# A windowed linear-attention layer: reciprocal denominators spread by transfers through memory and multiplied in by GpSimd, in place of matrix products and VectorE

## The chip, the core and the metric

The kernel runs on one core of one Trainium2 chip. The metric is the device time of one execution in microseconds (us); lower is better. Each line number is that of the kernel before, unless it is said to be of the changed kernel.

## The reference, cut to what matters

The network has two layers on an image of 256 channels and 64 x 64 pixels. Only layer 0 is touched. It is a linear attention with eight heads of 32 channels, over boxes of three sizes around each pixel:

```python
q = sigmoid(Wq x); k = sigmoid(Wk x); v = (Wv x) / |Wv x|        # x group-normed
for w in (1, 2, 4):                                              # box side 64, 32, 16
    wk, wkv = box(integral(k)), box(integral(k * v))             # sums over the box
    attn = einsum('bdhw,bdfhw->bfhw', q, wkv)                    # 32 channels of a head
    norm = einsum('bdhw,bdhw->bhw', q, wk)                       # one number a head and pixel
    outs.append(attn / (norm[:, None] + 1e-06))                  # <- the division
x = x + Wout @ concat(outs) + bout
```

Layer 1 (attention over all pixels, then a mixture of experts) follows and is the same in both kernels.

## The kernel before

The 4096 pixels are kept as 8 vertical strips (`NCH`) of 512 pixels (`CH`). The heads are done in two groups of four (`KC` = 2, loop at L744), since four heads fill 128 partitions. For each group `prepare` (L304) makes q, k, v, the box sums of k and, from them, all denominators of the group: the tile `den`, 128 x 512, whose row 32·(i mod 4) + 4·(2w + i div 4) + h holds the denominators of window w, strip i and head h. L526 adds 1e-6 and L527 takes all reciprocals at once, into the tile `rec`.

`attend` (L581) then works the three windows in the order w = 2, 1, 0, with reaches r = 1, 2, 4 (box half-sides in cells of 8 pixels). A window with r > 1 begins with a **band part** (L593 to L657: four bands b, products of 64 rows), and each window has a **strip part** (L660 to L708: eight strips ix). Both go in steps. One step makes for each of four heads a 128 x 512 (or narrower) product of k and q in a PSUM bank `sc` (L609, L678; six banks, four to a step). `masked` (L545) multiplies it by a mask into the tile `sm` (twelve buffers, so three steps): VectorE does so straight from PSUM for heads 0 and 2, and for head 3 in every second step; head 1, and head 3 in the other steps, are copied to `sm` by ScalarE (L554) and multiplied there by GpSimd (L558). Two steps later TensorE multiplies v by the four `sm` (L640, L694). A strip's sum goes to the tile `raw` (L704, VectorE, or L706, ScalarE, for r = 1). There is one buffer of `raw`.

When a window is done its divisions and projections are put into the list `chores` (L737 to L741), and each step of the next window pops one (`step_done`, L538); before the next window writes `raw` again, and at the end of the group, `finish` does what is left. A **division** (L714) treats two strips: for each, TensorE multiplies a 0/1 matrix of the constants (`spread`) by 32 rows of `rec`, which puts each head's reciprocal on that head's 32 rows in a PSUM bank (L718), and VectorE multiplies `raw` by the bank (L725). A **projection** (L727) treats one strip: four products of `raw` with the output weights `woT` (L731), added to the residual `t` by VectorE (L735).

Each engine runs its instructions in an order fixed when the kernel is built, and waits in that order. The builder may place an instruction earlier on its engine than the program writes it, where its inputs are expected to be ready. SyncE's queue (SP) issues the DMAs concerned here: the weights (L203, L205), the constants (L126) and the image rows (L285).

Of the kernel before, what the change touches and what calls it, by code (L numbers as in the profile page):

```python
# [22 lines left out]
F32 = mybir.dt.float32  # L23
# [7 lines left out]
P = 128  # L31
C = 256
KC = C // P
N = 4096
NT = N // P
CH = 512
NCH = N // CH
IMG = 64
SW = 8
BH = 16  # L40
NB = IMG // BH
CELL = SW * SW
D = 32
GRP = 8
REACH = (4, 2, 1)
NW = len(REACH)
# [14 lines left out]
    "k": {"sums": NCH // 4 * NW * D, "spread": NCH // 4 * NW * P, "before8": CH, "sides": NB * (SW + IMG + 1)},  # L61
# [9 lines left out]
def constants():  # L71
# [15 lines left out]

# [3 lines left out]
    col = np.arange(P)[None, :]  # L91
    out[:, _AT["spread"]] = np.concatenate([p[:, None] % D == 4 * n + col // D for n in ns], 1)
# [19 lines left out]
def tile_conv_attn_hybrid(ctx: ExitStack, tc: tile.TileContext, a: dict, out: bass.AP):  # L112
# [27 lines left out]
    def tok(i):  # L140
        return slice(P * i, P * (i + 1))
# [44 lines left out]
    with ExitStack() as phase:  # L186
# [9 lines left out]
        big = phase.enter_context(tc.tile_pool(name="c_big", bufs=1))  # L196

        def weights(g):

            gs = slice(P * g, P * (g + 1))  # L200
            w3 = big.tile([P, KC, 3, P], F32, tag="w3", name="w3")
            for n, name in enumerate(("wqT", "wkT", "wvT")):
                nc.sync.dma_start(w3[:, :, n, :], a[name][:, gs].rearrange("(k p) o -> p k o", p=P))  # L203
            woT = big.tile([P, NW, C], F32, tag="woT", name="woT")
            nc.sync.dma_start(  # L205
                woT, a["woutT"].rearrange("(w g p) o -> p w g o", g=KC, p=P)[:, :, g, :]
            )
            return w3, woT

        with (  # L210
# [27 lines left out]
            first = weights(0)  # L238
# [65 lines left out]
        def prepare(g, prep, ps):  # L304
# [4 lines left out]
            w3, woT = weights(g) if g else first  # L309
# [217 lines left out]
            nc.vector.reciprocal(rec, rec)  # L527
# [15 lines left out]
        turns = [0]  # L543

        def masked(work, scs, used, pieces):  # L545


            turns[0] += 1
            sms = []
            for h, sc in enumerate(scs):  # L550
                sm = work.tile([P, CH], F32, tag="sm", name="sm", bufs=12)
                src, engine = sc, nc.vector
                if h == 1 or h == 3 and turns[0] % 2:
                    nc.scalar.copy(sm[:, :used], sc[:, :used])  # L554
                    src, engine = sm, nc.gpsimd
                for at, n, mk in pieces:
                    to, of = (z[:, at : at + n].rearrange("p (m n) -> p m n", n=mk.shape[-1]) for z in (sm, src))
                    engine.tensor_mul(to, of, mk.unsqueeze(1).to_broadcast(list(to.shape)))  # L558
                sms.append(sm)
            return sms  # L560
# [20 lines left out]
        def attend(g, work, ps, qk, v, ssum, rec, woT):  # L581
# [6 lines left out]
            for w in (2, 1, 0):  # L588
# [125 lines left out]
                def division(ix, raw=raw, w=w):  # L714

                    for i, by in ((ix, score()), (ix + 1, score())):
                        at, n = slice(D * (i % 4), D * (i % 4 + 1)), NCH // 4 * w + i // 4
                        nc.tensor.matmul(  # L718
                            by,
                            ck["spread"][at, P * n : P * (n + 1)],  # L720
                            rec[at, :],
                            start=True,
                            stop=True,
                        )
                        nc.vector.tensor_mul(raw[:, i, :], raw[:, i, :], by)  # L725
# [18 lines left out]
        for g in range(KC):  # L744
            with tc.tile_pool(name="c_prep", bufs=1) as prep, psum("c_ps1", 2) as ps:
                of = prepare(g, prep, ps)
            with tc.tile_pool(name="c_work", bufs=1) as work, psum("c_ps2", 1) as ps:
                attend(g, work, ps, *of)
# [753 lines left out]
```

## Time and profile before

| | |
|---|---|
| median of three runs | 2935.82 us (2933.38 to 2937.23) |
| the profiled execution's own time | 2937.02 us |
| its span | 2935.2 us, so 1.82 us lie around it |
| layer 0, group 0: `attend`, first product to last | 142.6 to 527.3 us of the span |
| layer 0, group 1: the same parts | 643 to 1029 us |
| reach 1, strip part (group 0) | 144.2 to 232.3 us |
| reach 2, band part; strip part | 232.3 to 301.6; 301.6 to 370.5 us |
| reach 4, band part; strip part | 370.5 to 447.0; 447.0 to 508.1 us |
| last divisions and projections of the group | 508.1 to 527.4 us |
| mean granted TensorE clock | 0.974 of full speed |

In the lines of the profile, L718 is line 718 of the kernel; an entry such as `ps_sc<-rec,cstk` names the tile written and those read; PE is TensorE (PEld its weight loads), DVE VectorE, ACT ScalarE, POOL GpSimd. A float32 product appears as two matmul records. "Idle before" is the time for which the engine had nothing to run just before, and the name behind the arrow is what it waited for. The matmul ends are modelled, so that a TensorE that shows as busy throughout may still hide short waits.

### The profile page before, as it was taken

To read this page: it belongs to the slowest core of one execution; us is meant where nothing else is said; L and a number is where in the kernel's file an instruction comes from. 1 tells how busy PE (TensorE), PEld (TensorE's weight loads), DVE (VectorE), ACT (ScalarE), POOL (GpSimd) and SP (SyncE) were. 2 spreads that over 40 slices of the span, in tenths; PEclk is the share of its full clock that TensorE was granted. 3 is DMA by queue.
4 is the path that set the end of the run, shared out by engine and by line. 5 is a ranking of instruction groups with operands and counts; after the bars stand their busy time and mean duration, and the time that the engine had idled before them with its cause. 6 is when DMAs were issued, how large, how long until landed. Compare 5 with 4: busy or idle time off the path is not lost. (4 is left out here: it accounts for less than half of the span.)

```text
span 2935.2 us, 63107 instructions
## 1 busy us (share of the span) xinstructions
PE 2794.7 (95%) x26358; PEld 1352.3 (46%) x26358; DVE 2083.2 (71%) x3005; ACT 1533.0 (52%) x2134; POOL 720.3 (25%) x816
## 2 busy tenths in 40 slices
PE   6899999989999989999999999999999699999996
PEld 5466442735644354222222222222222268888884
DVE  5776768577677877999999999999999821111113
ACT  3242323124233213888888888888888622222222
POOL 1085858119485621000000000000000022222220
PEclk9999999999999999999999999999999879999997
DMA  5000000000000000000000000000000155555555
GB/s 142 6 3 3 2 3 2 7 1 3 4 2 3 1 19 1 5 5 5 5 5 5 5 5 5 5 5 5 5 5 5 53 182 200 191 189 195 192 196 198
DMA packets 97930, 137.35 MB, mean 47 GB/s; under 512 B 18242, under 2 KB 79272, under 8 KB 97636
## 3 DMA queue, kind: packets, MB, share of 16 engines
q1 hardware_dynamic: 82360, 105.31, 10.9%
q0 software_dynamic: 6912, 18.88, 2.2%
q10 hardware_dynamic: 8364, 9.02, 0.9%
q8 instruction: 210, 3.44, 0.5%
q14 instruction: 84, 0.69, 0.1%
HBM read 115.07 MB, written 18.12 MB: 45 GB/s over the span
## 5 line engine op out<-in xcount | busy, mean ns | idle before, releaser
L1001 ACT ACTIVATE pe<-ps_two 128x1024 f32<-128x1024 f32 x1024 | 993.1, 1022 | 150.0 <-PE ps_two L991 145.4
L1008 DVE TENSOR_TENSOR total<-total,pe 128x1024 f32<-128x1024 f32 x928 | 1058.2, 1217 | 0.0
L991 PE MATMUL ps_two<-qk 32*128 32x512 f32 x4096 | 629.1, 639 | 3.6 <-POOLq L946 1.9
L959 PE MATMUL ps_acc<-pe,v 128*32 128x512 f32 x4096 | 546.4, 605 | 0.1
L554 ACT COPY sm<-ps_sc 128x384 f32<-128x384 f32 (+4 forms) x486 | 232.4, 512 | 459.5 <-PE ps_sc L678 276.4
L558 POOL TENSOR_TENSOR sm<-sm,mask 128x192 f32<-128x192 f32 (+3 forms) x460 | 380.2, 861 | 231.6 <-ACT sm L554 231.0
L991 PEld LDWEIGHTS ps_two<-qk 32*128 32x128 f32 x4096 | 204.8, 183 | 418.7 <-PE ps_two L991 222.2
L558 DVE TENSOR_TENSOR sm<-ps_sc,mask 128x384 f32<-128x384 f32 (+3 forms) x708 | 324.2, 518 | 91.7 <-PE ps_sc L678 90.2
L1417 ACT ACTIVATE hid<-ps_hp,cols 128x256 f32<-128x256 f32 x288 | 136.4, 473 | 382.8 <-PE ps_hp L1416 382.0
L1266 POOL MEMSET on<- 128x256 f32 x1 | 0.3, 311 | 1175.1 <-PE ps_den L959 1175.1
L959 PEld LDWEIGHTS ps_acc<-pe,v 128*32 128x32 f32 x4096 | 80.7, 108 | 389.4 <-issue 376.2
L1416 PE MATMUL ps_hp<-xe,w 128*128 128x256 f32 x1152 | 257.0, 381 | 0.0
L1423 PE MATMUL ps_yp<-w,hid 128*128 128x256 f32 x1152 | 254.6, 379 | 0.0
L678 PE MATMUL ps_sc<-qk 32*128 32x192 f32 (+3 forms) x2688 | 245.3, 446 | 5.2 <-DVE sm L558 2.9
L1423 PEld LDWEIGHTS ps_yp<-w,hid 128*128 128x128 f32 x1152 | 216.4, 190 | 28.1
L1416 PEld LDWEIGHTS ps_hp<-xe,w 128*128 128x128 f32 x1152 | 208.5, 190 | 42.1 <-ACT hid L1417 5.0
L694 PE MATMUL ps_acc<-sm,v 128*32 128x192 f32 (+3 forms) x2688 | 216.6, 423 | 0.8 <-POOL sm L558 0.8
L1395 DVE TENSOR_SCALAR xe<-ps_tp,cols 128x256 f32<-128x256 f32 x72 | 35.9, 540 | 248.8 <-PE ps_tp L1391 228.7
L558 POOL TENSOR_TENSOR sm<-sm,ycut 128x384 f32<-128x384 f32 (+4 forms) x150 | 150.7, 1025 | 140.4 <-ACT sm L554 140.2
L678 PEld LDWEIGHTS ps_sc<-qk 32*128 32x128 f32 x2688 | 126.4, 186 | 124.0 <-DVE sm L558 70.4
L1425 DVE TENSOR_TENSOR y<-ps_yp,b 128x256 f32<-128x256 f32 x72 | 30.6, 425 | 208.1 <-PE ps_yp L1423 208.1
L558 DVE TENSOR_TENSOR sm<-ps_sc,ycut 128x512 f32<-128x512 f32 (+4 forms) x250 | 127.7, 562 | 64.8 <-PE ps_sc L609 62.7
(231 smaller groups left out, 2252.5 us busy)
## 6 DMA issues: line engine op xcount, KB each, us to landing
w<-in_L_ffn_W SPq DMA_DIRECT2D x72, 1024.0 KB
b<-in_L_ffn_b SPq DMA_DIRECT2D x36, 128.0 KB
rows<-in_x SPq DMA_DIRECT2D x16, 256.0 KB
zrows<-z SPq DMA_DIRECT2D x4, 1024.0 KB
y<-yrows SPq DMA_DIRECT2D x8, 512.0 KB
y<-yrows ACTq DMA_DIRECT2D x8, 512.0 KB
rec<-recs SPq DMA_DIRECT2D x60, 64.0 KB
x<-in_x ACTq DMA_DIRECT2D x4, 512.0 KB
```

The source lines that it names most:

```text
L554: nc.scalar.copy(sm[:, :used], sc[:, :used])
L558: engine.tensor_mul(to, of, mk.unsqueeze(1).to_broadcast(list(to.shape)))
L678: nc.tensor.matmul(scs[h][:, at : at + n], kT[hs[h], tok(i)], qT[hs[h], CH * ix + CELL * c0 : CH * ix + CELL * c1], start=True, stop=True, ...
L694: nc.tensor.matmul(acc[hs[h], CELL * c0 : CELL * c1], v[:, i, hs[h]], sms[h][:, at : at + n], start=not begun[0], stop=last and at == plac ...
L959: nc.tensor.matmul(to[D * hd : D * (hd + 1), :], lhsT(hd), rhs[:, hd, :], start=start, stop=stop, skip_group_check=True,)
L991: nc.tensor.matmul(sc[hd // 2][:, hd % 2, :], qk[hs, 1, g, tok(i)], qk[hs, 0, g, chunk(qc)], start=True, stop=True,)
L1001: nc.scalar.activation(pe[:, pair, :], s, AF.Exp, scale=C**-0.5)
L1008: add = nc.vector.tensor_add(to, first[:, pair, :] if i == 1 else to, pe[:, pair, :])
L1395: nc.vector.tensor_scalar(xe[:, k, :], tp[:, k, :], cols[:, gain], cols[:, shift], op0=ALU.mult, op1=ALU.add,)
L1416: nc.tensor.matmul(hp, w1[:, k, tok(n)], x_now[:, k, :], start=k == 0, stop=k == KC - 1)
L1417: nc.scalar.activation(hid[:, n, :], hp, AF.Gelu, bias=cols[:, n : n + 1])
L1423: nc.tensor.matmul(yp, hid[:, n, tok(j)], w2[:, n, :], start=n == 0, stop=n == NH - 1)
```

## The change

Five things differ.

1. The constants lose the matrix `spread` (768 columns).
2. `prepare` ends at the addition of 1e-6. The reciprocal is done in four pieces of 128 columns, as the first four chores of `attend`; each is placed on VectorE behind the last mask product issued so far.
3. The fifth chore, `turn_over`, writes `rec` (256 KB) to a tile `recs` in device memory and begins to fetch. A fetch is two DMAs on SP; each reads the four rows of one strip, every row 32 times, into one half of the tile `by` (128 x 512 floats, 256 KB, a half). `by` has two buffers; a division issues the next fetch.
4. A division is two multiplications on GpSimd, `raw` by `by`, both in SBUF. The two products and the two PSUM banks go.
5. The weights are split: q, k, v weights of the second group are asked for before the first group's `attend`, the output weights of a group at the start of its `prepare`.

```diff
-            nc.vector.reciprocal(rec, rec)
...
+            recs = dram.tile([P, CH], F32, name="recs")
+            windows = (2, 1, 0)
+            order = [(w, ix) for w in windows for ix in range(0, NCH, 2)]
+            held = []
+
+            def fetch():
+                if order:
+                    w, ix = order.pop(0)
+                    by = work.tile([P, 2, CH], F32, name="by", bufs=2)
+                    for i in (ix, ix + 1):
+                        row = D * (i % 4) + 4 * (NCH // 4 * w + i // 4)
+                        nc.sync.dma_start(
+                            by[:, i - ix, :],
+                            recs[row : row + 4, :].unsqueeze(1).to_broadcast([4, D, CH]),
+                        )
+                    held.append(by)
+
+            def turn_over():
+                nc.sync.dma_start(recs, rec)
+                for _ in range(2):
+                    fetch()
+
+            def reciprocal(z):
+
+                with tc.issue_after(latest[0]):
+                    nc.vector.reciprocal(z, z)
+
+            for i in range(4):
+                chores.append((NCH, lambda i=i: reciprocal(rec[:, tok(i)])))
+            chores.append((NCH, turn_over))
...
-                    for i, by in ((ix, score()), (ix + 1, score())):
-                        at, n = slice(D * (i % 4), D * (i % 4 + 1)), NCH // 4 * w + i // 4
-                        nc.tensor.matmul(
-                            by,
-                            ck["spread"][at, P * n : P * (n + 1)],
-                            rec[at, :],
-                            start=True,
-                            stop=True,
-                        )
-                        nc.vector.tensor_mul(raw[:, i, :], raw[:, i, :], by)
+                    by = held.pop(0)
+                    for i in range(2):
+                        nc.gpsimd.tensor_mul(raw[:, ix + i, :], raw[:, ix + i, :], by[:, i, :])
+                    fetch()
...
+            if g + 1 < KC:
+                w3 = weights(g + 1)
```

In the changed kernel as built, GpSimd's order shows where its multiplications stand. They are not in the next window: each stands in the strip part of its own window, one a strip, two steps behind the strip's last one. Three masks (two steps) follow the seventh multiplication of reach 1, one mask the seventh of reach 2, three masks the seventh of reach 4; the eighth stands behind the window's last mask in all three. The order of the other products on TensorE, and of the masks on all engines, is the same as before.

## The prediction

> **What bounds it now.** I read the stage table first (busy time of each engine by stretch), then the groups with shapes kept apart, then the timeline of each stage. Group 0's three strip parts and its end:
>
> ```profile
> 144.20:232.30 88.10, 86.43 (x1390) 51.84 (x1389) 68.48 (x155) 35.55 (x72) 76.86 (x110) 0.96 0.01 2
> 301.60:370.50 68.90, 68.90 (x851) 29.10 (x848) 54.06 (x127) 27.01 (x56) 60.10 (x72) 1.00 0.01 2
> 447.00:508.10 61.10, 60.92 (x542) 15.69 (x540) 48.89 (x87) 25.08 (x50) 53.15 (x48) 1.00 0.01 2
> 508.10:527.40 19.30, 17.76 (x84) 12.85 (x81) 16.48 (x26) 0.00 (x0) 0.00 (x0) 1.00 0.00 0
> ```
>
> Columns: stretch, its length, then PE, PEld, DVE, ACT, POOL busy, clock, DMA share, GB/s. TensorE is busy throughout, VectorE for 78 to 80%. But GpSimd, 25% of the whole span on the page, is busy for 87% of each strip part, and it is the engine that gets the new work. What that means for one multiplication, the groups tell:
>
> ```profile
> L558 POOL TENSOR_TENSOR sm<-sm,mask 128x512 f32<-128x512 f32 x92 | 116.3, 1280 | 19.4 <-ACT sm L554 19.4
> ...
> L725 DVE TENSOR_TENSOR raw<-raw,ps_sc 128x512 f32<-128x512 f32 x48 | 30.6, 683 | 8.9 <-PE ps_sc L718 8.9
> ...
> L718 PE MATMUL ps_sc<-rec,cstk 32*128 32x512 f32 x96 | 26.8, 640 | 0.1
> ...
> L336 POOL TENSOR_TENSOR sq<-v 128x512 f32<-128x512 f32 x16 | 16.6, 1039 | 77.3 <-DVE v L335 77.3
> ...
> L527 DVE RECIPROCAL rec<-rec 128x512 f32<-128x512 f32 x2 | 6.7, 3353 | 0.1
> ...
> L342 DVE RECIPROCAL ss<-ss 128x64 f32<-128x64 f32 x4 | 2.2, 553 | 0.1
> ```
>
> Last, GpSimd's own timeline, one run of masks a line: in reach 1, 2 and 4 it rests 0.29 us in 3.78, 1.16 in 11.16, and 0.82 in 7.45:
>
> ```profile
> 159.65 3.49 POOL L558 TENSOR_TENSOR sm<-sm,mask 128x192 f32<-128x192 f32 x5 [0.29 <-ACT sm L554]
> ...
> 348.51 9.99 POOL L558 TENSOR_TENSOR sm<-sm,mask 128x256 f32<-128x256 f32 x12 [1.16 <-ACT sm L554]
> ...
> 495.82 6.64 POOL L558 TENSOR_TENSOR sm<-sm,mask 128x512 f32<-128x512 f32 x6 [0.82 <-ACT sm L554]
> 503.27 3.75 POOL L558 TENSOR_TENSOR sm<-sm,mask 128x512 f32<-128x512 f32 x3 [0.81 <-ACT sm L554]
> ```
>
> **The change, part by part** (one group; the second repeats the first, its stages being equal within 0.4 us but the reach 4 strip part, whose stretch I cut 1 us wider).
>
> *Price of a multiplication.* It reads two tiles and writes one of them, as the masks do: 1.28 us. The other bound is 1.04 us, of L336, which writes elsewhere and reads one tile twice. I take 1.28, since the masks' form is its own; from 0.24 us less, 21 on the path in a group would give back 5.0 us.
>
> *Removed products, band parts.* TensorE goes on to its next product 1.06, 1.43, 1.05 and 1.05 us after the divisions at 233.3, 235.6, 250.0 and 260.7 begin: 4.6 us. The first two stand among the first three steps, where without them the third step still waits for VectorE to free banks, so I take 4.2. In reach 4 they cost 1.06, 1.65, 1.06, 1.06 (371.1, 373.0, 385.4, 395.1); I take 4.1 of 4.8. No GpSimd multiplication but a window's eighth (1.28 us) is left in a band part, and it ends as that part's first masks come in (234.2 before).
>
> *Removed products, end of group.* From 508.06, where the first division starts, to 527.34, where the next `prepare` begins, is 19.3 us. What is left is eight projections, one every 1.73 us (VectorE's additions start 0.86 us apart, two to a projection), 0.25 to fill and 0.79 until VectorE has freed the banks: 14.9. Gain 4.4. The eighth multiplication is needed only for the last projection.
>
> *VectorE's products* (48 of 0.683 us) go at nothing: in these stages VectorE itself waits for TensorE's scores, so TensorE's products hide them. Were VectorE the bound, they would give back up to 16.4 us a group.
>
> *Reciprocal.* 3.35 us of VectorE stand between the denominators and the first mask; TensorE has two steps' banks and runs dry. Four pieces of 128 columns cost, between 553 ns for 64 and 3353 for 512 (6.25 ns a column), 0.95 us each, one behind each of the first four steps' masks. I followed the queue: scores of step 0 ready at 143.7, masks of steps 0 to 3 end at 144.9, 147.8, 149.9 and 152.7 (before: about 155.2), last piece 153.7. So TensorE would be 2 us earlier, but the next term takes that back.
>
> *The transfers, and the new wait.* GpSimd's first multiplication stands behind the masks of step 5, which with the earlier start end near 157.1 (159.4 before). It waits for: piece 4 (153.7), the write of `recs`, a fetch. Behind it on GpSimd are all masks from step 6 on, and TensorE needs those two steps later. Price from layer 1, which does such a thing with less data:
>
> ```profile
> 1237.23 1.73 SPq L1060 DMA_DIRECT2D rec<-recs  x4
> ```
> ```profile
> 1238.20:1239.20 1.00, 1.00 (x12) 0.16 (x9) 1.00 (x2) 1.00 (x2) 0.00 (x0) 1.00 0.40 141
> 1239.20:1240.20 1.00, 1.00 (x8) 0.25 (x8) 1.00 (x2) 0.81 (x1) 0.00 (x0) 1.00 0.40 129
> ```
>
> Four reads of 64 KB, issued from 1237.2, move from 1238.5 to about 1240.2: 1.3 us to start, some 135 GB/s, so 256 KB take 3.3 us. The write: `dens<-rec` (8 KB) holds the next DMA for 1.77 us from issue (1224.78 to 1226.55); 256 KB more at 238 GB/s (image rows, 29 to 31 us) add 1.1: 2.9. With 0.1 us for each hand-over the first half of `by` lands at 153.7 + 0.1 + 2.9 + 0.1 + 3.3 = 160.1. Nearest rows bound it at 157.1 (hidden) and, with the 135 GB/s of one queue taken for both transfers and half of it for the read, 163. [...]
>
> Later fetches are issued a strip or more ahead (7 us at least) and are hidden. Queued on SP behind them is only the second group's `woT`, which before waited there until 526.6 anyway; splitting the weights costs nothing.
>
> *Reach 1.* From 160.1 GpSimd has the first multiplication, 38 steps (19 pairs of 3.50 us) and six more multiplications before its last mask: 160.1 + 66.5 + 7 x 1.28 = 235.6, if it never rests again. Before, the last mask ended at 231.2. **Loss 4.4** (earlier start counted). With the fetch hidden it would be 1.4.
>
> *Reach 2.* Masks are 60.4 us from 303.5; with seven multiplications GpSimd cannot end before 372.9 (before: 369.7): at least 3.2. The multiplication after a strip's second step also delays the masks of the third and fourth, needed within 0.2 us of their end now: some 0.5 us of TensorE wait a strip that reappears as rest of GpSimd. **Loss 4.1.**
>
> *Reach 4.* A multiplication comes where GpSimd rests, 0.1 us after the rest begins (`raw` is summed at 495.08, masks end at 495.0). 1.28 + 0.1 - 0.82 = 0.56 a strip, seven times, less 0.1 of slack: **loss 3.8.**
>
> Sum: -4.2 - 4.1 - 4.4 + 4.4 + 4.1 + 3.8 = -0.4 us a group, -0.8 in both: 2937.02 becomes 2936.2. The profiled execution is 1.2 above the median of the runs, so about **2935.0** there. Faster or slower by 0.2% is 5.9 us, about what a measurement of this kernel can tell from no change; my forecast is no change.
>
> **Rivals.**
> 1. *GpSimd has room after all; faster.* For: the multiplications are off every engine shown as full, and VectorE and TensorE lose work. Against: 87% busy. With 1.04 us (-5.0) and the fetch half hidden (-1.5), a group gains 6.9: 2922. With only one of them: 2925 to 2932.
> 2. *GpSimd cannot use its rests; slower.* The rests are waits for ScalarE's copies, which wait for TensorE's scores. If TensorE's waits for `sm` push the scores back too, the rests come again behind each multiplication, and each costs its full 1.28 instead of the remainder: at most 7 x 1.28 = 9.0 in each strip part, against 1.4, 4.1 and 3.8 counted net of fetch, +17.7 a group, 2970. Against: the next two steps' scores are out when TensorE waits, so GpSimd has masks queued. It decides from one fifth of that (3.4 us a group), 2942 and up. A fetch landing after 163 would come to the same: each us costs one us a group.
> 3. *The wait of the first multiplication is hidden, the rest as counted; faster*: -3.4 a group in all, 2929. For: a pipeline of 38 steps lies behind it. Against: five things in a row (above) must be done by 157.1.
>
> That the change does not do what it says is excluded by the built order.
>
> **How the numbers follow.** Sums near zero (2929.9 to 2941.7): 0.42, with likeliest 2935.0. Faster: rival 1 0.19, rival 3 0.08, together 0.27. Rival 2 and late fetches: 0.31. The known stages can hardly gain more than counted, while each GpSimd wait not seen here adds; hence slower a little above faster. Range 2923 to 2947: rival 1 nearly whole below; above, up to a quarter of rival 2's bound with a late fetch.
>
> **What would show it.** Right: in the strip parts of reach 1 and 4 GpSimd above 97% busy with rests near zero, TensorE's weight loads waiting for `sm` of GpSimd (now 6.3 us in all), strip parts longer by about 4 us each; band parts shorter by 4, the end of a group 15 us long. The first multiplication shows a wait for DMA of about 3 us. Wrong: multiplications of 1.04 us; strip parts unchanged; a DMA wait before later multiplications; or GpSimd resting as often as now while the strip parts grow by 9.

## The result, and the profile after

The changed kernel takes 2938.43 us (median, 2937.41 to 2938.55), the kernel before, run beside it, 2936.57 (2933.38 to 2940.0): a ratio of 1.0005 with a 95% interval of 0.9992 to 1.0018. That is no change, as forecast (2935.0). Its profiled span is 2935.6 us, against 2935.2.

To find where the time went I cut each group's `attend` at TensorE's first instruction of each part. In us, group 0 / group 1:

| part | before | after | difference | forecast |
|---|---|---|---|---|
| strip part, reach 1 | 89.65 / 90.06 | 93.76 / 93.04 | +4.1 / +3.0 | +4.4 |
| band part, reach 2 | 69.27 / 69.09 | 69.95 / 68.35 | +0.7 / -0.7 | -4.2 |
| strip part, reach 2 | 68.96 / 69.84 | 72.78 / 72.82 | +3.8 / +3.0 | +4.1 |
| band part, reach 4 | 75.57 / 76.07 | 71.19 / 71.15 | -4.4 / -4.9 | -4.1 |
| strip part, reach 4 (to its last product) | 62.06 / 62.06 | 65.29 / 65.29 | +3.2 / +3.2 | +3.8 |
| end | 19.20 / 24.25 | 14.80 / 20.46 | -4.4 / -3.8 | -4.4 |
| sum | 384.71 / 391.37 | 387.77 / 391.11 | +3.1 / -0.3 | -0.4 |

Outside, group 0 began 1.9 us earlier (among all runs told here that start lies anywhere from 140.0 to 143.4, so I count this as chance), the second `prepare` took 0.1 more and layer 1 0.6 less: -1.9 + 3.1 + 0.1 - 0.3 - 0.6 = +0.4, the difference of the spans.

The stage table of the changed kernel, with the columns as in the prediction (the fifth busy time is GpSimd's):

```profile
142.00:234.50 92.50, 87.88 (x1390) 50.91 (x1388) 69.28 (x158) 35.81 (x73) 84.71 (x117) 0.98 0.09 33
304.50:377.30 72.80, 71.47 (x863) 29.54 (x855) 54.27 (x127) 27.02 (x56) 68.40 (x79) 1.00 0.07 24
448.40:513.70 65.30, 64.94 (x553) 17.22 (x545) 49.39 (x89) 25.09 (x50) 62.59 (x57) 1.00 0.05 17
513.70:528.50 14.80, 14.05 (x67) 12.05 (x64) 11.65 (x18) 0.00 (x0) 1.28 (x1) 1.00 0.01 1
```

GpSimd went from 87% of the strip parts to 92, 94 and 96%. The groups, with shapes kept apart, first one line of the kernel before, then the changed kernel:

```profile
L694 PEld LDWEIGHTS ps_acc<-sm,v 128*32 128x32 f32 x2688 | 66.7, 109 | 119.4 <-issue 94.5 <-POOL sm L558 6.3 <-ACT raw L653 2.6
```
```profile
L729 PEld LDWEIGHTS ps_acc<-sm,v 128*32 128x32 f32 x2688 | 70.6, 109 | 140.8 <-issue 94.0 <-POOL sm L559 29.0 <-ACT raw L688 2.6
L753 POOL TENSOR_TENSOR raw<-raw,by 128x512 f32<-128x512 f32 x48 | 61.0, 1271 | 20.3 <-DMA by<-recs 8.4 <-DVE raw L739 8.0 <-ACT raw L741 3.7
...
L618 DVE RECIPROCAL rec<-rec 128x128 f32<-128x128 f32 x8 | 7.6, 946 | 0.0
```

TensorE's weight loads now wait 29.0 us for GpSimd's masks (6.3 before); a multiplication takes 1.271 us, a piece of the reciprocal 0.946. GpSimd's timeline in reach 1 has the first multiplication's wait. Behind it GpSimd, in group 0, rests twice (0.31 and 0.75 us, before 167.5), and then not once until its last multiplication:

```profile
158.22 1.27 POOL L753 TENSOR_TENSOR raw<-raw,by 128x512 f32<-128x512 f32 x1 [4.01 <-DMA by<-recs]
...
172.09 10.39 POOL L559 TENSOR_TENSOR sm<-sm,mask 128x192 f32<-128x192 f32 x15
182.44 1.26 POOL L753 TENSOR_TENSOR raw<-raw,by 128x512 f32<-128x512 f32 x1
183.67 10.40 POOL L559 TENSOR_TENSOR sm<-sm,mask 128x192 f32<-128x192 f32 x15
```

TensorE's timeline at the end of group 0 shows eight projections in one run where there were divisions between them:

```profile
513.67 14.08 PE L760 MATMUL ps_sc<-woT,raw 128*128 128x256 f32 x64
528.54 16.67 PE L324 MATMUL ps_two<-w,act 128*128 128x256 f32 x76 [0.78 <-DVE t L764]
```

And at the start of the reach 2 band part, where the forecast failed, it shows a longer wait that nothing in the profile released ("issue"), then a projection of 3.31 us where others take 1.99. First the kernel before, then the changed kernel:

```profile
241.97 0.54 PE L640 MATMUL ps_acc<-sm,v 64*32 64x192 f32 x10 [0.63 <-issue]
242.44 1.99 PE L731 MATMUL ps_sc<-woT,raw 128*128 128x256 f32 x8
```
```profile
240.67 1.09 PE L675 MATMUL ps_acc<-sm,v 64*32 64x128 f32 x46
243.64 0.80 PE L675 MATMUL ps_acc<-sm,v 64*32 64x192 f32 x2 [1.88 <-issue]
244.37 3.31 PE L760 MATMUL ps_sc<-woT,raw 128*128 128x256 f32 x8
```

The stage table microsecond by microsecond gives the clock (third from the end) and the share of the DMA engines (second):

```profile
156.00:157.00 1.00, 1.00 (x24) 0.42 (x16) 0.74 (x2) 0.59 (x1) 0.00 (x0) 1.00 0.26 98
...
162.00:163.00 1.00, 1.00 (x6) 0.50 (x8) 0.00 (x0) 0.00 (x0) 1.00 (x2) 0.50 0.27 100
...
242.00:243.00 1.00, 0.00 (x0) 0.00 (x0) 0.00 (x0) 0.00 (x0) 0.49 (x1) 1.00 0.26 102
...
244.00:245.00 1.00, 1.00 (x4) 0.54 (x3) 0.00 (x0) 0.00 (x0) 0.00 (x0) 0.50 0.06 16
```

A fetch keeps a quarter of the DMA engines busy at 98 to 102 GB/s. After each of two longer waits of TensorE in group 0 (1.48 us in reach 1, and the 1.88 us above) the granted clock is 0.50 for some 3 us. In group 1 the same waits (1.84 and 1.73 us) left it at 1.00. Group 1 took 0.7 us less in reach 1, which fits; that the clock is the reason is not shown.

### The profile page after: what moved, and what is told of

Same layout as the page of the kernel before. It is cut to its first block, busy times and chain, and to the rows that moved or that the text cites. A ratio compares the mean times of both kernels' runs of the same rounds, so it can differ in the third digit from the quotient of the medians.

```text
span 2935.6 us, 63064 instructions
## 1 busy us (share of the span) xinstructions
PE 2781.2 (95%) x26262; PEld 1342.8 (46%) x26262; DVE 2054.4 (70%) x2963; ACT 1533.0 (52%) x2134; POOL 777.4 (26%) x864
## 3 DMA queue, kind: packets, MB, share of 16 engines
q8 instruction: 210, 3.44, 0.5%
## 4 chain that ended last, share of the span: by engine, by line
PE 57%; DMA 1%; DVE 1%; ACT 1%; issue 1%; POOL 0%; DVEq 0%; SPq 0%; POOLq 0%; ACTq 0%
PE ps_two L1022 20%; PE ps_acc L990 17%; PE ps_yp L1454 8%; PE ps_hp L1447 8%; PE ps_den L971 1%; DMA y<-yrows 1%; PE ps_den L990 1%; PE ps_acc L1371 1%; ACT z L1255 1%; PE ps_tp L1422 1%; DMA xs<-zrows,source 0%; DVE total L1039 0%; DMA yrows<-y,target 0%; DVE t L1491 0%; DVE rec L1068 0%
## 5 line engine op out<-in xcount | busy, mean ns | idle before, releaser
L729 PE MATMUL ps_acc<-sm,v 128*32 128x192 f32 (+3 forms) x2688 | 232.4, 420 | 10.2 <-POOL sm L559 10.2
L1426 DVE TENSOR_SCALAR xe<-ps_tp,cols 128x256 f32<-128x256 f32 x72 | 35.8, 539 | 250.3 <-PE ps_tp L1422 228.6
L559 DVE TENSOR_TENSOR sm<-ps_sc,ycut 128x512 f32<-128x512 f32 (+4 forms) x250 | 127.6, 562 | 74.2 <-PE ps_sc L644 71.4
```

What stands on the lines that cost most here:

```text
L559: done = engine.tensor_mul(to, of, mk.unsqueeze(1).to_broadcast(list(to.shape)))
L729: nc.tensor.matmul(acc[hs[h], CELL * c0 : CELL * c1], v[:, i, hs[h]], sms[h][:, at : at + n], start=not begun[0], stop=last and at == plac ...
L1426: nc.vector.tensor_scalar(xe[:, k, :], tp[:, k, :], cols[:, gain], cols[:, shift], op0=ALU.mult, op1=ALU.add,)
```

## The experiments

The same cuts for each run, group 0 / group 1:

| run | reach 1 strip | reach 2 band | reach 2 strip | reach 4 band | reach 4 strip | end | time |
|---|---|---|---|---|---|---|---|
| 1 no division | 86.9 / 86.9 | 68.0 / 66.8 | 68.8 / 68.8 | 71.2 / 71.7 | 62.3 / 62.3 | 14.8 / 20.4 | 2909.2 |
| 2 `by` in place | 89.0 / 89.0 | 68.1 / 66.3 | 72.8 / 72.8 | 71.6 / 71.4 | 65.3 / 65.3 | 14.8 / 20.4 | 2926.7 |
| 3 GpSimd later | 86.9 / 86.9 | 67.7 / 69.0 | 68.8 / 69.0 | 71.2 / 71.1 | 65.3 / 65.3 | 14.8 / 20.7 | 2916.5 |
| 4 VectorE | 86.9 / 87.0 | 70.9 / 73.4 | 68.8 / 69.8 | 77.4 / 77.6 | 66.0 / 66.0 | 14.8 / 20.2 | 2937.2 |
| 5 all later | 86.9 / 86.9 | 67.6 / 69.1 | 68.8 / 69.0 | 71.6 / 71.3 | 62.1 / 62.1 | 19.8 / 20.6 | 2915.2 |
| 6 pieces alone | 86.9 / 86.9 | 70.1 / 70.7 | 69.2 / 69.8 | 75.6 / 76.2 | 62.1 / 62.0 | 19.2 / 24.3 | 2933.1 |
| 7 fetches alone | 88.8 / 89.3 | 67.5 / 68.2 | 69.1 / 69.1 | 71.4 / 71.7 | 62.3 / 62.1 | 14.8 / 20.5 | (2979.1) |
| 8 rows apart | 91.2 / 91.1 | 67.5 / 67.6 | 72.8 / 72.8 | 71.2 / 71.7 | 65.3 / 65.3 | 14.8 / 20.7 | 2934.1 |
| 9 `side` freed | 86.9 / 86.9 | 69.0 / 68.2 | 68.8 / 69.0 | 71.3 / 71.7 | 62.0 / 62.1 | 15.0 / 20.9 | 2912.4 |
| 10 spread | 86.9 / 86.9 | 66.4 / 65.8 | 68.8 / 69.0 | 73.7 / 73.3 | 62.0 / 62.1 | 15.0 / 20.8 | 2910.9 |
| 11 spread, reach 2 | 86.9 / 86.9 | 65.8 / 65.5 | 68.8 / 69.0 | 71.2 / 71.1 | 62.1 / 62.1 | 15.0 / 20.8 | **2906.1** |
| 12 double boxes | 86.9 / 86.9 | 85.7 / 83.8 | 68.8 / 69.0 | 87.4 / 86.5 | 62.1 / 62.1 | 15.0 / 21.1 | 2974.1 |

The parts are those of each run's profiled execution, the time is the median. Strip parts with the same work agree between runs within 0.3 us (but group 1's reach 2 part is 69.8 in runs 4 and 6, as in the kernel before, and 68.8 to 69.1 elsewhere without multiplications); the reach 2 band part scatters by about 1 us a run, so one value of it proves little. Layer 1 takes 1899 to 1902 us in all but run 7 (1964.6: other values reach it there, and its work depends on them), so the time of run 7 is not compared. The diffs are against the changed kernel unless they say otherwise.

**1. No division.**

```diff
-                nc.sync.dma_start(recs, rec)
...
-                    held.append(by)
+                    held.append(None)
...
-                    for i in range(2):
-                        nc.gpsimd.tensor_mul(raw[:, ix + i, :], raw[:, ix + i, :], by[:, i, :])
```

> Leaves out the division: no write of the reciprocals, no fetch of `by`, no multiplication; the rest and TensorE's order stay as in the changed kernel. It asks what the multiplications and transfers cost together, stage by stage (stretches cut at the first TensorE instruction of each part; group 0 of the changed kernel: strip part of reach 1 93.8 us, band part of reach 2 70.0, strip part of reach 2 72.8, band part of reach 4 71.2, strip part of reach 4 65.2, end 14.9). Theory A (GpSimd is what the strip parts wait for, the transfers are what the reach 2 band part waits for): the strip parts fall to those of the kernel before, 89.7, 69.0 and 62.0, and the reach 2 band part to 65 to 66.5, as the prediction had counted; in all about 15 us a group, 2908. Theory B (the reach 2 band part is bound by the loading of TensorE's instructions whether or not anything else moves, so the removed products were worth nothing there): strip parts as in A, the band part stays at 68 to 70, 2915. Theory C (TensorE's order without the products is what costs, not GpSimd): all parts stay, within 1 us, 2935.

Measured 2909.2, ratio 0.990 (0.9884 to 0.9915) to the kernel before. GpSimd's timeline has its old rests again:

```profile
163.50 3.49 POOL L559 TENSOR_TENSOR sm<-sm,mask 128x192 f32<-128x192 f32 x5 [0.30 <-ACT sm L555]
167.28 3.50 POOL L559 TENSOR_TENSOR sm<-sm,mask 128x192 f32<-128x192 f32 x5 [0.29 <-ACT sm L555]
```

The strip parts are as in theory A (reach 1 even 3 us below the kernel before: see run 6), so C falls. The reach 2 band part lies between A and B: 67.4 on average, 1.8 below the kernel before where 4.2 were forecast. So more than half of that miss is there without any transfer or multiplication.

**2. `by` in place.**

```diff
-                nc.sync.dma_start(recs, rec)
...
+            fixed = work.tile([P, 2, CH], F32, name="by", bufs=1)
+            nc.scalar.copy(fixed, qT[:, : 2 * CH].rearrange("p (i n) -> p i n", n=CH))
...
-                    held.append(by)
+                    held.append(fixed)
```

> Leaves out the reciprocals' transfers: the multiplications stay on GpSimd, each where it was, but they read one tile that is filled once and stays in SBUF (so they multiply by something else). It tells the transfers from the multiplications. Theory A (the transfers delay the reach 2 band part and the first multiplication): reach 1 strip part 93.8 less about 2.9 (the wait of 4.0 us gone, of which GpSimd's old rests would return some), 90.5 to 91.5; reach 2 band part 65 to 67; strip parts of reach 2 and 4 unchanged at 72.8 and 65.2; about 6 us a group, 2926. Theory B (instruction loading bounds that band part by itself): the same but the band part at 68 to 70, about 3 us a group, 2933. Theory D (GpSimd's last multiplication, which waits for ScalarE's copy and then delays the first masks, is what the band part lost): as B in time, but the TensorE wait named issue at the band part's start (1.9 us in group 0, 1.7 in group 1) is unchanged and the following parts too.

Measured 2926.7, ratio 0.996 (0.9945 to 0.9975). Against run 1 it gives the price of the multiplications alone: 2.1 us in reach 1, 4.0 in reach 2, 3.0 in reach 4, nothing in the band parts and at the end. Against the changed kernel it gives that of the transfers: 4.8 / 4.1 us in reach 1, and 1.9 / 2.1 in the reach 2 band part, the latter little more than that part's scatter. The time is theory A's, though reach 1 lies 1.5 us below what A gave. The wait named issue at the band part's start is 1.0 and 0.3 us instead of 1.9 and 1.7, so theory D falls.

**3. GpSimd later.** The multiplications of reach 1 and 2 go to the next band part.

```diff
+                    with tc.issue_after(latest[1]) if w else nullcontext():
                         for i in range(2):
                             nc.gpsimd.tensor_mul(raw[:, ix + i, :], raw[:, ix + i, :], by[:, i, :])
```

> The multiplications of the reach 1 and reach 2 windows are queued behind GpSimd's masks of the next band part's first steps; those of reach 4 stay where they are. Theory A (GpSimd has no rest in strip parts and much in band parts, where it is busy for about half of the time): strip parts of reach 1 and 2 fall to 89.7 and 69.0 us, that of reach 4 stays at 65.2, the band parts grow by 0 to 2 us each (two multiplications of 2.55 us stand between masks that TensorE needs about two steps later); 4 to 8 us a group faster, 2922 to 2930. Theory E (masks behind a pair of multiplications come too late for TensorE in the band parts too): band parts longer by 1.3 us or more for each pair, 5 us each, and nothing is gained, 2936 to 2941.

Measured 2916.5, ratio 0.9925 (0.9912 to 0.9939): more than theory A gave, because reach 1 also keeps what the pieces of the reciprocal gain. GpSimd's timeline in the reach 4 band part:

```profile
377.23 2.24 POOL L559 TENSOR_TENSOR sm<-sm,ycut 128x448 f32<-128x448 f32 x2 [1.05 <-ACT sm L555]
379.43 2.51 POOL L753 TENSOR_TENSOR raw<-raw,by 128x512 f32<-128x512 f32 x2
381.88 2.66 POOL L559 TENSOR_TENSOR sm<-sm,ycut 128x384 f32<-128x384 f32 x3
```

A pair stands between masks, and the part is as long (71.2 us) as without multiplications: here GpSimd had been resting anyway. The same work costs 6 us in these two strip parts (run 2 less run 1) and nothing in the reach 4 band part; the reach 2 band part (68.3 on average against 67.4 in run 1) differs by no more than its scatter.

**4. VectorE.**

```diff
-                        nc.gpsimd.tensor_mul(raw[:, ix + i, :], raw[:, ix + i, :], by[:, i, :])
+                        nc.vector.tensor_mul(raw[:, ix + i, :], raw[:, ix + i, :], by[:, i, :])
```

(for reach 1 and 2 behind `latest[0]`, VectorE's last mask)

> The multiplications by `by` are VectorE's, from SBUF: behind the next band part's first masks for reach 1 and 2, behind each strip's sum for reach 4. GpSimd gets nothing but masks, as in the kernel before. Theory A (the price was GpSimd's; VectorE, 80% busy in these stages, has room, and did the same products from PSUM before in 0.68 us): strip parts 89.7, 69.0 and 62.0, band part of reach 4 71.2, end about 15; the reach 2 band part between 66 and 70, by what the transfers do to instruction loading; 11 to 15 us a group faster than the changed kernel, 2909 to 2916, and faster than the kernel before by 0.7 to 0.9%. Rival F (VectorE is nearly as tight as GpSimd: 48 multiplications of 0.7 us, half of them on the path): 17 us less gain, 2926 to 2932.

Measured 2937.2, ratio 0.9992 (0.9983 to 1.0001): both expectations fail. Against run 1 the reach 4 strip part is 3.7 us longer and the band parts 2.9 to 6.6. The profile shows two things that lengthen the band parts; what each cost was not separated. One is in the timeline, VectorE's products beside GpSimd's masks, with a product of the reach 4 strip part as the last line:

```profile
386.55 1.14 POOL L559 TENSOR_TENSOR sm<-sm,ycut 128x448 f32<-128x448 f32 x1 [2.42 <-ACT sm L555]
386.89 1.34 DVE L754 TENSOR_TENSOR raw<-raw,by 128x512 f32<-128x512 f32 x1
387.64 1.58 POOL L559 TENSOR_TENSOR sm<-sm,ycut 128x448 f32<-128x448 f32 x1
...
466.01 0.69 DVE L754 TENSOR_TENSOR raw<-raw,by 128x512 f32<-128x512 f32 x1
```

With both inputs in SBUF the product takes 0.69 us while GpSimd rests. Begun inside a mask, it takes 1.34: the mask keeps its 1.14 us, the product ends 0.54 us behind the mask's end, and the next mask, begun inside the product, takes 1.58. From PSUM, as in the kernel before, the product took 0.683 beside the same masks. The other is the granted clock:

```profile
372.80:379.80 7.00, 6.91 (x150) 4.65 (x151) 3.39 (x7) 0.48 (x1) 2.39 (x3) 0.51 0.23 80
```

It is 0.50 for 3.4 to 6.8 us near the start of all four band parts of this run. In the reach 4 strip part, with the clock at 1.00 and the products at 0.69, eight of them still cost 3.7 us: VectorE's 80% was no more room than GpSimd's 87%.

**5. All later**, and **9. `side` freed.** All multiplications behind the window's last mask, `by` fetched by single strips into seven buffers; run 9 adds the last three lines.

```diff
+                    for i in (ix, ix + 1):
+                        with tc.issue_after(latest[1]):
+                            nc.gpsimd.tensor_mul(raw[:, i, :], raw[:, i, :], held.pop(0))
+                        fetch()
...
-            nc.vector.memset(side, 0.0)
+            with tc.issue_after(added[0]) if g else nullcontext():
+                nc.vector.memset(side, 0.0)
```

> As the run with the later multiplications, but those of reach 4 too are queued behind the window's last GpSimd mask, and `by` is fetched strip by strip into seven buffers (so that seven strips of the last window are there when it ends). The first multiplication then stands between the last mask, which ends about 1 us before the last product, and the first projection; the others take 1.28 us each where a projection takes 1.73. Theory A (GpSimd in the strip parts is the whole price): strip part of reach 4 65.3 to 62.3, end 14.8 to between 15 and 16.5, the rest as in that run: 1.5 to 2.8 us a group less than its 2916.5, 2911 to 2914. Rival: the end takes as much as the strip part gives (first multiplications or fetches late), 2916 to 2918.

Measured 2915.2, ratio 0.9922 (0.9908 to 0.9935): the rival's side. The strip part gave 3.2, but group 0's end took 5.0 back. In the timeline an instruction of the next `prepare`, which takes over memory that GpSimd's multiplications still use, stands in VectorE's queue ahead of the projections' additions:

```profile
509.08 0.11 DVE L433 MEMSET side<- 128x65 f32 x1 [6.74 <-POOL raw L748]
...
509.79 9.55 PE L755 MATMUL ps_sc<-woT,raw 128*128 128x256 f32 x36 [3.00 <-DVE t L759]
```

> As the run with all multiplications later, but the next group's first VectorE instruction that takes over GpSimd's memory (the clearing of `side` in `prepare`) is queued behind the last projection's addition. In that run it stood in VectorE's queue ahead of group 0's additions and held them and TensorE until GpSimd's eight multiplications were over (VectorE waited 6.7 us, TensorE 3.0): the end took 19.8 us instead of 14.8, in group 1, with no group behind it, 20.6 as ever. Theory A (that queueing is all that kept the gain of 3.2 us in the reach 4 strip part from the time): end of group 0 15 to 16 us, strip parts 86.9, 68.8, 62.0; 2910 to 2912. Rival (what is moved behind is late in `prepare` by as much): end short, the second `prepare` longer by 3 to 5 us, 2914 to 2916.

Measured 2912.4, ratio 0.991 (0.9893 to 0.9926); end of group 0 15.0, the second `prepare` 117.0 against 116.9 in run 5: theory A, within 0.4 us.

**6. The pieces alone**, in the kernel before.

```diff
-            nc.vector.reciprocal(rec, rec)
...
+            for i in range(4):
+                chores.append((NCH, lambda i=i: reciprocal(rec[:, tok(i)])))
```

> The kernel before (products and all) with one part of the change alone: the reciprocal in four pieces of 128 columns behind the first four steps' masks. Theory (the whole reciprocal of 3.35 us kept TensorE from its third step, and without the later wait for a fetch that gain stays): strip part of reach 1 from 89.7 and 90.1 to 86.9 us, as it was in the runs in which nothing waits for the fetch, all other parts as before: 2.9 us a group, 2931 to 2932. Rival (the pieces cost VectorE the same 3.8 us a little later, and the gain of those runs came from the products' absence): 89 to 90, 2936 to 2938.

Measured 2933.1, ratio 0.9982 (0.9972 to 0.9991). Reach 1 falls by 2.8 and 3.2 us, to 86.9. The theory's size came (86.9), but not by its reason alone. First TensorE's timeline in the kernel before, where VectorE's masks stand behind the whole reciprocal, then in this run:

```profile
146.39 3.44 PE L678 MATMUL ps_sc<-qk 32*128 32x256 f32 x24 [1.45 <-DVE sm L558]
```
```profile
143.77 1.13 PE L687 MATMUL ps_sc<-qk 32*128 32x256 f32 x16 [0.34 <-DVE sm L557]
145.61 0.92 PE L687 MATMUL ps_sc<-qk 32*128 32x192 f32 x12 [0.71 <-DVE sm L557]
```

In these lines the waits for the masks differ by only 0.4 us (1.45 against 0.34 and 0.71). What differs more is the granted clock, in the stage table of the kernel before (both groups) and then of this run:

```profile
146.50:153.40 6.90, 6.90 (x60) 4.53 (x64) 3.59 (x10) 1.54 (x3) 3.51 (x6) 0.51 0.01 2
648.30:655.10 6.80, 6.80 (x60) 3.57 (x59) 3.71 (x9) 1.54 (x3) 4.39 (x6) 0.50 0.00 0
```
```profile
146.00:153.00 7.00, 6.68 (x101) 3.76 (x97) 7.00 (x16) 2.31 (x5) 5.90 (x9) 1.00 0.01 2
```

In the kernel before TensorE runs at half clock for 6.8 us behind that wait, in both groups. As an estimate from these rows that costs up to 3.4 us, against the 2.8 and 3.2 gained. So most of what the pieces gain seems to be the clock; no run keeps the two apart.

The reach 2 band part is 0.8 and 1.6 longer, with nothing changed in it: its waits named issue went from 4.8 us to 5.3 and 6.2.

**7. Fetches alone.**

```diff
-                        nc.gpsimd.tensor_mul(raw[:, ix + i, :], raw[:, ix + i, :], by[:, i, :])
+                        nc.gpsimd.tensor_mul(raw[:, ix + i, :8], raw[:, ix + i, :8], by[:, i, :8])
```

> Leaves out nearly all of the division: the transfers are all there, and each multiplication is cut to 8 of its 512 columns, so that it waits for its fetch and frees its buffer as in the changed kernel but costs next to nothing. Against the run without a division it adds the transfers alone. Theory A (the transfers make the reach 2 band part late): that part 69.9 and 68.4 us as in the changed kernel, not 68.0 and 66.8; reach 1 strip part 88.5 to 91 (the first multiplication still waits for its fetch); strip parts of reach 2 and 4 at 68.8 and 62.3; 2915 to 2921. Theory D (the last multiplication before the band part makes it late): band part 66.8 to 68.0.

Reach 1 as expected (88.8 / 89.3: the wait costs 2.0 / 2.4 by itself, and more where GpSimd has no rests to catch up in). The reach 2 band part is 67.5 / 68.2: theory A's 69.9 / 68.4 did not come, theory D's 66.8 to 68.0 nearly. So what run 2 put down to the transfers there is not theirs alone: it may be multiplication and transfer together, or the scatter. This stays open.

**8. Rows apart.**

```diff
-                            by[:, i - ix, :],
-                            recs[row : row + 4, :].unsqueeze(1).to_broadcast([4, D, CH]),
+                        for h in range(4):
...
+                                by[D * h : D * (h + 1), i - ix, :],
+                                recs[row + h : row + h + 1, :].to_broadcast([D, CH]),
```

> The changed kernel with each strip's fetch issued as four transfers, one for each head's row to its 32 partitions, instead of one transfer with the four rows outermost; the bytes are the same. In the changed kernel the fetches run at 98 to 104 GB/s with a DMA share of 0.26, which is about 4 of 16 engines. Theory G (the four outermost rows confine a transfer to four engines): share above 0.5, the first multiplication's wait 4.0 us to 1.5 to 2.5, strip part of reach 1 shorter by 2 to 3 us, the reach 2 band part by up to 2; 2929 to 2934. Rival H (the rate is set elsewhere, say by the one queue): share and wait stay, and the fourfold number of issues adds to them, 2937 to 2941.

Measured 2934.1, ratio 0.9987 (0.9978 to 0.9996). From the stage table, and from GpSimd's timeline:

```profile
155.00:156.00 1.00, 1.00 (x18) 0.67 (x19) 0.31 (x2) 0.11 (x1) 0.00 (x0) 1.00 0.69 141
```
```profile
156.52 1.28 POOL L754 TENSOR_TENSOR raw<-raw,by 128x512 f32<-128x512 f32 x1 [2.56 <-DMA by<-recs]
```

Theory G: the share is 0.57 to 0.69 instead of 0.26, the rate 137 to 150 GB/s, the wait 2.56 us instead of 4.01, reach 1 shorter by 2.5 / 2.0. The rate rose less than the share; what holds it there is not shown. The reach 2 band part is 2.4 / 0.8 shorter, and the time just above theory G's range.

**10. Spread**, against run 9; **11. spread in reach 2 only.**

```diff
-                for b in (1, 2, 0, 3) if r > 1 else ():
+                for b in (1, 0, 2, 3) if r > 1 else ():
...
-                                finish(NCH)
+                                finish(NCH if b < 2 else NCH + 1)
...
-                    for b in range(0, NB, 2):
+                    for b in bs:
...
+                for i in range(NCH) if w else ():
+                    chores.append((NCH + 1, lambda i=i, f=projection: f(i, (2,))))
```

> As the run before it in this list, with one thing more: half of the projections (those of token blocks 2 and 3) leave the first band of a band part and go one by one to the steps of the next bands, until the band that overwrites their blocks; the bands come in the order 1, 0, 2, 3. The work is the same. Theory N (in the second half of the reach 2 band part TensorE is bound by the loading of its instructions, about 3.7 us for every 128 products with their weight loads, while the first half, with the long products of the projections, leaves that loading idle; so time saved in the first half is given back in the second): spread evenly the loads keep up, TensorE's waits named issue go from about 6 to 7 us to under 3 us, the part from 67.6 and 69.1 to 62 to 65.5 us, 2900 to 2906 in all. Rival O (those waits only show where the chain of scores and masks leaves TensorE idle anyway): the part stays within 1 us, 2910 to 2913. The reach 4 band part, where no such waits are seen, stays at 71 either way.

Measured 2910.9, ratio 0.9906 (0.9889 to 0.9922), little from run 9. But the parts moved: reach 2 band 2.7 and 2.4 us shorter, issue waits 7.1 / 6.5 to 5.3 / 5.0; reach 4 band 2.3 and 1.7 longer. That is theory N's direction at less than its size (62 to 65.5 and under 3 us of waits were expected).

> As the run with the projections spread, but only in the reach 2 band part (order of the bands 1, 0, 2, 3); the reach 4 band part, which became 2.3 and 1.7 us longer there, keeps its projections in its first band and the order 1, 2, 0, 3. Theory (spreading helps where TensorE waits for its instructions, 2.7 and 2.4 us, and costs where it doesn't): band parts 66 and 71.4 us, 2906 to 2909 in all, and the best of these kernels. Rival (the longer reach 4 band part follows from what the reach 2 window left, not from the order): 73.5 again, 2910 to 2912.

Measured 2906.1, ratio 0.988 (0.9864 to 0.9897): the best of these kernels, 1.2% faster than the kernel before. The reach 4 band part is back at 71.2 and 71.1, so the rival falls: there it was the order that cost.

**12. Double boxes**, against run 9; the sums of boxes count twice.

```diff
-                                for u, ix in ((u, ix) for u in range(2) for ix in range(NCH)):
+                                for n, u, ix in ((n, u, ix) for n in range(2) for u in range(2) for ix in range(NCH)):
...
-                                            start=ix == 0,
+                                            start=ix == 0 and n == 0,
```

> The kernel with all multiplications later and `side` freed, with TensorE's products of the box sums (128 short ones a band, of 64 columns, 15.5 ns each, on bands' starts) done twice, so that the sums are counted twice: 512 products and 512 weight loads more in each band part, 8.0 us of TensorE's own time at the 1.99 us that 128 of them took. Only layer 0's parts are read, since other values may give layer 1 other work. Theory N (loading of instructions at 3.7 us for 128 products bounds the second half of the reach 2 band part): that part grows by more than TensorE's own time, 2 to 3.7 us in the first band and 3 times 3.7 in the second half, from 69.0 and 68.2 to 81.5 to 84 us, while the reach 4 band part, which leaves the loading room, grows by 8.0, from 71.3 and 71.7 to 79.3 to 79.9. Rival O (the waits named issue are slack of the chain of scores and masks): both parts grow by 8.0 or less, the reach 2 part to 77 or less, because the added products fill some of those waits.

The reach 2 band part grew by 16.7 and 15.6 us, to 85.7 and 83.8: one above theory N's range, one inside it, both far above rival O's 77. After the last projection, where the sum is not mixed with other work, by 11.2 and 10.4, for which theory N had 11.1 and TensorE's own time 6. TensorE's timeline there, the lines with a wait only:

```profile
294.06 1.99 PE L661 MATMUL ps_acc<-qk,ssum 32*32 32x64 f32 x128 [1.56 <-issue]
297.52 0.52 PE L661 MATMUL ps_acc<-qk,ssum 32*32 32x64 f32 x19 [1.47 <-issue]
...
301.24 0.84 PE L673 MATMUL ps_acc<-sm,v 64*32 64x192 f32 x19 [0.65 <-issue]
...
305.25 0.76 PE L642 MATMUL ps_sc<-qk 32*64 32x192 f32 x19 [0.48 <-issue]
...
308.98 1.99 PE L661 MATMUL ps_acc<-qk,ssum 32*32 32x64 f32 x128 [1.29 <-issue]
...
312.70 0.52 PE L661 MATMUL ps_acc<-qk,ssum 32*32 32x64 f32 x19 [1.74 <-issue]
```

The waits stand exactly 128 matmul records apart, whatever matmul it is, and 3.46 to 4.01 us apart. The added work did not fill the waits (they rose from 7 to 14 and 13 us), so rival O falls. The reach 4 part, meant as the undisturbed one, grew by 16.0 and 14.8 instead of 8.0 and now shows 6.4 and 5.7 us of the same waits: there too, 256 short matmuls in a row outrun what feeds them. (In each of the four band parts 3.4 us at a clock of 0.50 are in the growth too, up to 1.7 us each.)

That these are waits for instructions, the traces show. Queue q8 carries instructions; here are its line on the page of run 9, its line on the page of this run, and the DMA rates of this run from 290 to 316 us, in slices of 0.65 us, where q8 is the only queue that moves anything:

```profile
q8 instruction: 210, 3.44, 0.5%
```
```profile
q8 instruction: 226, 3.70, 0.5%
```
```profile
GB/s 0 0 25 0 0 0 0 25 0 0 0 0 0 25 0 0 0 0 25 0 0 0 0 0 0 25 0 0 0 0 25 0 0 0 0 0 25 0 0 0
q8 instruction: 7, 0.11, 1.9%
```

Run 12 has 4,096 matmul and weight-load records more than run 9, and 16 packets of 16.4 KB more: 256 instructions a packet. Each 25 in the row is one packet, and one stands ahead of each wait's end. In all fourteen traces the reach 2 band parts have 233 waits named issue (over 0.15 us); each of them ends 1.19 to 1.61 us after a packet of q8 has been moved, and the next packet starts 1.03 us or more after the wait has ended.

## Why the prediction was right, step by step

- **Price of a multiplication**: 1.28 forecast, 1.271 measured. Right.
- **Reciprocal**: pieces 0.95 forecast, 0.946 measured; TensorE 2 us earlier, 3.0 measured (run 6). Low by one, and for a reason that the working left out: it counts waits alone, while its own stage table has a clock of 0.96 in reach 1, which is the 6.8 us at half clock that run 6 loses.
- **The first wait**: landing forecast at 160.1; measured 158.22, and 1.85 for the earlier start gives 160.07. The sum hit, its terms did not: the last piece ended 1.1 earlier, the write took 2.2 (2.9), the read 5.3 (3.3). I took the 135 GB/s of layer 1's reads, which move at a share of 0.40; the fetch moved at 98 to 102 GB/s and a share of 0.26, which is about four engines of 16, and with the rows apart the share rose to 0.57 to 0.69 (run 8).
- **Reach 1** +4.4: +4.1 and +3.0. Made of -3.0 (pieces), +2.1 (multiplications, run 2 less run 1) and +4.8 / +4.1 (fetch). The working had about -2.3, +3.7 and +3.0 (1.4 with the fetch hidden, 4.4 with it). So the fetch cost more than I counted, the multiplications cost less and the earlier start gained more: that the sum came near is luck.
- **Reach 2 and 4 strip parts**: 4.1 and 3.8 forecast; 4.0 and 3.0 by run 2 less run 1. (Reach 2 shows +3.8 and +3.0 because the two groups of the kernel before were 0.9 us apart there, not within the 0.4 that the prediction says.) The mechanism is shown by run 3: the same multiplications elsewhere cost nothing.
- **Reach 4 band part and end**: -4.1 and -4.4; -4.4 / -4.9 and -4.4 / -3.8. Right.
- **Reach 2 band part**: -4.2 forecast; +0.7 / -0.7. This is the step that failed: "The first two stand among the first three steps, where without them the third step still waits for VectorE to free banks, so I take 4.2." The products themselves were sized well: up to the end of the projections run 1 is 3.1 and 4.8 us shorter than the kernel before (33.55 and 31.97 against 36.69 and 36.76). But what follows, in which nothing was removed, became 1.9 and 2.5 longer (34.46 and 34.83 against 32.58 and 32.33). Over the runs the scatter is less of a doubt: without the products (runs 1, 2, 3, 5, 7, 8 and 9, both groups) the first half takes 33.4 us on average and the second 34.5; with them (the kernel before and run 6) 36.8 and 33.0. So 3.4 is gained and 1.5 given back. In the second half TensorE is fed one block of 128 matmuls with their weight loads every 3.5 to 4.0 us, and coming earlier it only waits more. In the changed kernel's group 0 a second loss comes on top: its first half takes 35.8 us, where those runs take 32.0 to 34.0, with the 1.88 us wait while `by` was being moved and the half clock after it; group 1's 33.5 lies among them. That the second half is bound so is shown by runs 12 and 11, and that it is the loading of instructions by the packets of q8 (run 12).
- **VectorE's products at nothing**: run 4 is no test of it, since it moved them to other operands.
- **Rivals**: 1 (GpSimd has room) is wrong for the strip parts and right for the band parts, which I had not asked. 2 is excluded: 2.1 to 4.0 us a strip part for the multiplications (run 2 less run 1), not 9. Run 2, which has no fetch to wait for, comes nearest to 3: 2926.7, where I had 2929.
- **Signs**: GpSimd was to be above 97% busy in reach 1 and 4; 92% (with the 4 us wait) and 96%. That wait, forecast at about 3, is 4.01. TensorE's waits for `sm` rose from 6.3 to 29.0 us, as said.

So five of the six parts moved the way and about the amount that was forecast, one of them (reach 1) by errors that cancel. The sixth was 4.9 and 3.5 us too good; the -0.8 of the prediction was +2.8 in the parts, of which the earlier start, which is chance, hid 1.9 in the profile. No change was forecast for the right reason, that GpSimd's price in the strip parts eats what TensorE saves; that the number came within 3.4 us is partly luck.

## What to carry to other kernels

Before work is given to an idle engine, ask in which stage it rests: GpSimd, at 25% of the span, had no room in the stage where the scheduler put the multiplications and all the room needed in the next; moving them made a gain of 0.75% (run 3) out of none. A part with many short matmuls may be bound by how fast instructions come, as the reach 2 band part was here, which gave back 1.5 of the 3.4 us saved ahead of it; waits at equal counts of instructions (every 128 matmuls with 128 weight loads, run 12) were the sign. The clock column of a stage table is worth as much as the waits: in the kernel before, 6.8 us at half clock stood behind one wait of 1.45 us. And a queue that crosses a stage's end can hold the end up: in run 5 one instruction on VectorE waited 6.74 us there, and the end took 5.0 us more.

## What the runs showed of the hardware

- TensorE's instructions come through q8: on the page of the changed kernel it moves 3.44 MB in 210 packets, 16.4 KB each, and 4,096 instructions more took 16 packets more (run 12). The waits of run 12 come every 128 matmuls with 128 weight loads, 256 instructions. The waits named issue come to 4.8 us in the reach 2 band part of the kernel before, and to 14 in run 12.
- Two inputs in SBUF: VectorE's product takes 0.69 us alone, and 1.34 when it begins inside a GpSimd mask. In run 4 the mask begun first kept its 1.14 us, the product ended 0.54 us behind it, and the next mask, begun inside the product, took 1.58. What holds the second of the two back is not shown.
- In the changed kernel the granted clock fell to 0.50 for some 3 us after waits of 1.48 and 1.88 us in group 0, and stayed at 1.00 after waits of 1.84 and 1.73 us in group 1; in the kernel before it was 0.50 for 6.8 us behind a wait of 1.45 us, in both groups. These runs do not show what decides it.
